# Four chained layers on one core: the product of step sizes and u moves from GpSimd to VectorE in the second state-space layer

## The chip, the cores and the metric

The kernel runs on one core of a Trainium2 chip. A core has five engines with a queue each: TensorE (PE in the profile; its weight loads are PEld), VectorE (DVE), ScalarE (ACT), GpSimd (POOL) and SyncE (SP), which here only issues transfers between the chip's memory (HBM) and the core's SBUF. Matrix products go to a second on-chip memory, PSUM, which TensorE writes and which VectorE and ScalarE read and write. Each engine works through its own instructions in order; between engines, semaphores hold an instruction back until what it reads is there and what it overwrites has been read.

The metric is the device time of one execution in microseconds (us). Lower is better.

## The reference

The input is eight images of 384 channels and 32 x 32 positions. Four layers follow one another: a state-space layer, a layer of deformable convolutions, a second state-space layer with layer norm and a small two-layer network behind it, and a layer of shifted Gaussian samples. The change is in the third of them, the second state-space layer. For each image its core is this recurrence over 1024 positions, with 768 inner channels d and 16 states n:

```python
dbc = xc @ x_proj_w.T
dt, Bm, Cm = jnp.split(dbc, [dt_rank, dt_rank + d_state], axis=-1)
dt = softplus(dt @ dt_proj_w.T + dt_proj_b)
A = -jnp.exp(A_log)
def step(h, inp):
    dt_t, B_t, C_t, u_t = inp
    dA = jnp.exp(dt_t[..., None] * A)
    h = dA * h + (dt_t * u_t)[..., None] * B_t[:, None, :]
    y = jnp.einsum('bdn,bn->bd', h, C_t)
    return (h, y)
```

The factor `dt_t * u_t`, called du below, is what the change is about: one elementwise product of the step sizes dt and the convolved input u.

## The kernel before

Everything is 32-bit floating point. `ssm_layer` runs both state-space layers. It splits each image into two halves of 512 positions, called steps: 16 steps in a layer, and the second step of an image carries the state of the first. The 768 inner channels are six tiles of 128. The work on one tile in one step is a block, and a block has eight units, 0 to 7. A unit holds 32 channels times 4 states on the 128 partitions and two further states in its 1024 columns. So a layer has 16 x 6 x 8 = 768 units, run strictly one after another.

One unit i does this:

- `inputs` (L539, GpSimd): db = du times B, 128 x 1024, three buffers. It is issued three units ahead, so it waits until the scan three units before it has released its buffer.
- `decays` (L531, ScalarE): da = exp(dt times A) into PSUM, two instructions of 512 columns, two buffers, issued two units ahead.
- `scan` (L551, VectorE): the recurrence over da and db. In units 0, 2 and 5 of a block its result goes to a tile hs in SBUF, otherwise it stays in PSUM in place of da.
- `with_c`: the product with C. Units 0, 2 and 5 do it on GpSimd (L562), the other five on VectorE (L564).
- `keep_last` (L557, ScalarE): in the first step of an image, the last state. In the second step, GpSimd adds the carried state to the first column (`carry` L514, `add_carry` L524).
- `read_out` (L574, TensorE): sums the states into y, one or two units later.

Around the units lies all other work of the layer, placed by hand. `plan` writes, for each step, four lists (act, dve, pool, pe) with one slot per unit, and fills them with the closing of the block before, the projections and the convolution of the next step, the output projection and the two-layer network of the step before, and the softplus of the block two ahead. In each unit the loop then issues, in this order: the slot's act list, the scan, VectorE's product with C, keep_last, the decays two units ahead, the dve list, the inputs three units ahead with their carry additions, GpSimd's product with C, the pool list, the pe list. On an engine, the order of issue is the order of execution. The transfers on SyncE's queue also run in order; their order is set when the kernel is built, from what they depend on.

The softplus of a tile is spread over one block: `dt_proj` (TensorE, slot 2), `soft_exp` (ScalarE, slot 3), `soft_rest` (VectorE L464, slot 4, writes the tile sp_e), `soft_ln` (ScalarE, slot 5), and in slot 6 `soft_sum` on GpSimd: two sums that finish dt (L472, L473), then the product with u, written over sp_e (L474). In slot 7 `spread` stores dt and du to HBM (L493, SyncE) and loads them back in the layout of the units (dtb and dub, four loads each, L498). The first reader of dub is the inputs of the next block's first unit, issued in slot 5 of the block between. The tiles dt, sp_e and sp_w have one buffer each.

The first state-space layer does not use `soft_sum`: there TensorE adds the three parts of the softplus in PSUM, ScalarE copies dt out, and VectorE multiplies the PSUM tile with u (`soft_du`, L488). The switch is `PE_SUM = (0,)`.

Other lines that the text speaks of: in the second state-space layer, `ln_scale` (L348, VectorE) scales the layer norm, `down_take` (L660, VectorE) adds the network's output to the residual x, `norm_stats` (L308, VectorE) takes statistics of a newly loaded x (L301), `fetch_in` (L280) loads the projection weights winr two units before their use. In the convolution layer, a set-up piece adds two one-column tiles on VectorE (L1107) while GpSimd subtracts weights (L1224, L1226).

Of the kernel before, what the change touches and what calls it, by code (L numbers as in the profile page):

```python
# [10 lines left out]
ALU = mybir.AluOpType  # L11
# [91 lines left out]
class Net:  # L103
# [112 lines left out]
    def ssm_layer(self, li, src, dst, shift=None):  # L216
        tc, nc, ins = self.tc, self.nc, self.ins
        mlp = li == 2
        gp_c = GP_C[li]
        pe_sum = li in PE_SUM  # L220
        sel = self.cols[:, Q_SEL : Q_SEL + IP]
        with ExitStack() as ctx:
# [210 lines left out]
            def load_bc(s, p):  # L433
                bc = s["bc"][p] = p2.tile([P, 2, 2, TS], F32, name="bc", tag="bc", bufs=3)
                for i in range(NI):
                    nc.sync.dma_start(
                        out=bc[i * IP : (i + 1) * IP].rearrange("p t q l -> p (t q) l"),
                        in_=s["bcd"][i, p].partition_broadcast(IP),
                    )
# [29 lines left out]
            def soft_sum(s, j):  # L469
                dt = s["dt", j]  # L470
                s["du", j] = du = s["e"]
                nc.gpsimd.tensor_tensor(dt, dt, s["e"], ALU.subtract)  # L472
                nc.gpsimd.tensor_tensor(dt, dt, s["w"], ALU.add)  # L473
                nc.gpsimd.tensor_tensor(du, dt, s["u"][:, j, :], ALU.mult)  # L474

# [215 lines left out]
            def plan(prev, s, nxt):  # L693
                act, dve, pool, pe = queues = [[[] for _ in range(T + NU)] for _ in range(4)]

                def put(q, t, fn, *args):
                    if not args or args[0]:
                        q[t].append((fn, *args))

                for j in range(ND):  # L700
                    t = NU * j
                    put(dve, t + 2, close, *((s, j - 1) if j else (prev, ND - 1)))
                    tz = TZ[j]
                    put(pe, tz - 2, fetch_in, s, ND + j)
                    put(pe, tz, z_proj, s, j)
                    put(act, TG[j], gate, s, j)

                    n, k = (s, j + 2) if j + 2 < ND else (nxt, j + 2 - ND)
                    put(pe, t + 2, dt_proj, n, k)
                    put(act, t + 3, soft_exp, n, k)  # L710
                    put(dve, t + 4, soft_rest, n, k)
                    put(act, t + 5, soft_ln, n, k)
                    if pe_sum:
                        put(pe, t + 6, soft_add, n, k)
                        put(act, t + 7, soft_take, n, k)
                        put(dve, t + 7, soft_du, n, k)
                    else:
                        put(pool, t + 6, soft_sum, n, k)
                    put(pool, t + 7, spread, n, k)
                for i, t in enumerate(TS2):  # L720
                    put(act, t, silu, nxt, 3 * i, 3 * i + 3)
# [3 lines left out]
                t = 0 if nxt else 14  # L725
# [67 lines left out]
            with tc.manual_schedule(engines=ENGINES):  # L793
                s = steps[0]
# [24 lines left out]
                states()  # L819
                for j in range(2):  # L820
                    for fn in (dt_proj, soft_exp, soft_rest, soft_ln) + (
                        (soft_add, soft_take, soft_du) if pe_sum else (soft_sum,)
                    ) + (spread,):
                        fn(s, j)
                    load_bc(s, j)
# [8 lines left out]
                for i, (s, j, m) in enumerate(units):  # L834
                    c, t = divmod(i, T)
                    if t == 0:
                        queues = plan(
                            steps[c - 1] if c else None, s, steps[c + 1] if c + 1 < len(steps) else None
                        )
                        for k, q in enumerate(over or ()):  # L840
                            for i0, items in enumerate(q):
                                queues[k][i0][:0] = items
                        act, dve, pool, pe = queues
                        over = [q[T:] for q in queues]
# [1313 lines left out]
```

## Time and profile before

| | us |
|---|---|
| median of 3 runs | 8728.45 (8723.46 to 8728.67) |
| the profiled execution | 8722.48 |
| its span, first to last instruction | 8720.7 |
| GpSimd's 96 products L474, each | 1.26 to 1.28 |

The second state-space layer begins at about 5300 us of the span and its last units end near 8460 us. In that stretch of 3160 us the engines were busy for 2573 us (TensorE), 2767 us (VectorE), 2260 us (ScalarE) and 2886 us (GpSimd).

How to read the lines further down: a group's line has the source line, the engine, the operation, output and inputs with their shape, the count, then the busy time and the mean nanoseconds of one, then the engine's idle time just before these instructions and what ended it. A line of the timeline has the start, the duration, the engine, the line and operation, output and inputs, and in brackets the idle time before it and what ended that. A line of the view by stretches has the stretch, its length, the busy time of TensorE, its weight loads, VectorE, ScalarE and GpSimd (with counts of instructions), the granted clock of TensorE, the busy share of the transfer engines and GB/s.

### The profile page before, as it was taken

What the parts mean: (1) busy time and instruction counts of PE and PEld (TensorE: products, weight loads), DVE (VectorE), ACT (ScalarE), POOL (GpSimd) and SP (SyncE); (2) the same over time, 40 slices, a digit from 0 to 9 for tenths busy, and PEclk for the clock granted to TensorE, in tenths of its full rate; (3) what the DMA queues carried; (4) which work ended last, traced back from release to release, by engine and by line L of the source; (5) the groups of instructions that cost most, each with busy time, mean ns of one, the idle gap of its engine ahead of it and who ended that gap; (6) DMA issues with size and microseconds to landing.
All of it is one profiled execution on the core that took longest, in us unless ns stands there. A gap on an engine that the chain in (4) does not pass through costs nothing. (4 is left out here: it accounts for less than half of the span.)

```text
span 8720.7 us, 91254 instructions
## 1 busy us (share of the span) xinstructions
PE 7387.2 (85%) x29688; PEld 3825.2 (44%) x29688; DVE 7519.7 (86%) x8480; ACT 5832.6 (67%) x9518; POOL 5569.8 (64%) x3383
## 2 busy tenths in 40 slices
PE   7888888888886899999999985788888888888878
PEld 2232233223222788888787871233333333333323
DVE  6999999999997788988988895888988989888884
ACT  6777777777774556666666665676767777776761
POOL 6999999999998000000000005998998989898984
PEclk8899899889987999999999997898998899999989
DMA  4555555555553754565456434565666666565657
GB/s 126 126 126 123 120 124 125 118 122 125 125 126 99 186 133 110 130 166 127 103 148 159 122 76 122 131 153 144 156 156 156 149 147 153 141 157 142 154 152 152
DMA packets 796928, 1179.29 MB, mean 135 GB/s; under 512 B 260402, under 2 KB 413010, under 8 KB 762648
## 3 DMA queue, kind: packets, MB, share of 16 engines
q1 hardware_dynamic: 739444, 1157.23, 54.0%
q10 hardware_dynamic: 55540, 10.05, 0.7%
q0 software_dynamic: 1456, 6.07, 0.2%
q8 instruction: 237, 3.88, 0.2%
q14 instruction: 251, 2.06, 0.1%
HBM read 984.15 MB, written 188.98 MB: 135 GB/s over the span
## 5 line engine op out<-in xcount | busy, mean ns | idle before, releaser
L539 POOL TENSOR_TENSOR db<-dub,bc 128x1024 f32<-128x1024 f32 x1536 | 3606.2, 2357 | 369.1 <-DVE hs L551 169.1
L531 ACT ACTIVATE da<-dtb,vec 128x512 f32<-128x512 f32 x3072 | 2122.2, 691 | 610.5 <-DVE hs L564 407.9
L551 DVE TENSOR_TENSOR_SCAN da<-da,db 128x1024 f32<-128x1024 f32 x960 | 2193.2, 2285 | 130.5 <-ACT da L531 86.1
L472 POOL TENSOR_TENSOR dt<-dt,sp_e 128x512 f32<-128x512 f32 x96 | 122.3, 1274 | 2468.0 <-DMA bc<-bcd 2463.7
L1803 PE MATMUL wacc<-fsm,fxk 128*128 128x195 f32 (+21 forms) x10624 | 1574.9, 306 | 98.6 <-DVE fsm L1766 69.4
L1803 PEld LDWEIGHTS wacc<-fsm,fxk 128*128 128x128 f32 x10624 | 1481.2, 195 | 232.8 <-DVE fsm L1766 140.5
L551 DVE TENSOR_TENSOR_SCAN hs<-da,db 128x1024 f32<-128x1024 f32 x576 | 1315.3, 2283 | 195.6 <-POOL db L524 84.0
L562 POOL TENSOR_TENSOR hs<-hs,bc 128x1024 f32<-128x1024 f32 x576 | 1357.0, 2356 | 34.1 <-ACT st L557 34.1
L564 DVE TENSOR_TENSOR hs<-da,bc 128x1024 f32<-128x1024 f32 x960 | 1175.6, 1225 | 122.4 <-PE y L574 72.9
L574 PE MATMUL y<-hs,cols 128*32 128x512 f32 x6144 | 968.6, 649 | 282.5 <-POOL hs L562 260.1
L1766 DVE TENSOR_TENSOR fsm<-fhy,fhx 128x585 f32<-128x585 f32 (+39 forms) x3136 | 1011.2, 389 | 85.8 <-PE wacc L1803 77.0
L1749 DVE TENSOR_TENSOR fxk<-fxt,fwk 128x1024 f32<-128x1024 f32 (+1 forms) x688 | 813.4, 1182 | 9.7 <-DMA fxt<-fxd 8.7
L1726 ACT ACTIVATE fhy<-fpyx,cell 128x416 f32<-128x416 f32 (+10 forms) x832 | 422.4, 580 | 315.2 <-DVE fsm L1766 315.2
L574 PEld LDWEIGHTS y<-hs,cols 128*32 128x32 f32 x6144 | 189.1, 113 | 1002.4 <-issue 507.7
L651 PE MATMUL ps_m<-hid,wm 128*128 128x512 f32 x1152 | 549.9, 632 | 61.9 <-ACT hid L646 27.8
L632 PE MATMUL ps_h<-t,wm 128*128 128x512 f32 x1152 | 533.4, 607 | 56.5 <-DVE sp_e L464 24.2
L1709 ACT ACTIVATE fhx<-fpyx,cell 128x352 f32<-128x352 f32 (+9 forms) x640 | 344.5, 610 | 294.6 <-DVE fsm L1766 264.1
L364 PE MATMUL ps_in<-xn,winr 128*128 128x512 f32 x576 | 326.4, 713 | 176.6 <-ACT xn L353 127.0
L651 PEld LDWEIGHTS ps_m<-hid,wm 128*128 128x128 f32 x1152 | 226.8, 203 | 395.1 <-issue 283.5
L632 PEld LDWEIGHTS ps_h<-t,wm 128*128 128x128 f32 x1152 | 217.0, 194 | 376.6 <-issue 275.6
L583 PE MATMUL ps_z<-xn,winr 128*128 128x512 f32 x576 | 301.5, 672 | 47.7 <-DVE sp_e L464 47.7
L606 PE MATMUL ps_o<-u,wm 128*128 128x512 f32 x576 | 279.9, 636 | 41.5 <-DMA wm<-in_wout 36.3
(239 smaller groups left out, 9885.4 us busy)
## 6 DMA issues: line engine op xcount, KB each, us to landing
dtb<-dtd SPq DMA_DIRECT2D x768, 256.0 KB
dub<-dtd SPq DMA_DIRECT2D x768, 256.0 KB
fpyx<-fposd SPq DMA_DIRECT2D x104, 1024.0 KB
fxt<-fxd SPq DMA_DIRECT2D x96, 1024.0 KB
wm<-in_w SPq DMA_DIRECT2D x96, 768.0 KB
bc<-bcd SPq DMA_DIRECT2D x256, 256.0 KB
x<-x SPq DMA_DIRECT2D x73, 768.0 KB
dtd<-dt SPq DMA_DIRECT2D x192, 256.0 KB
```

Of the source, the lines that this page charges most:

```text
L531: nc.scalar.activation(da[:, i, :], s["dtb", j][:, k, :], AF.Exp, scale=na[:, j, n + i : n + i + 1])
L539: nc.gpsimd.tensor_tensor(db, du, s["bc"][p][:, 0], ALU.mult)
L551: nc.vector.tensor_tensor_scan(h1, da1, db1, 0.0, ALU.mult, ALU.add)
L562: nc.gpsimd.tensor_tensor(s["hs", m], s["hs", m], c, ALU.mult)
L564: nc.vector.tensor_tensor(hs_tile(s, m), s["da", m], c, ALU.mult)
L574: nc.tensor.matmul(s["y"][k * IP : (k + 1) * IP, :], sel, s["hs", p * NSUB + k][:, i, :], start=mlp and p == 0 and i == 0, stop=p == NQP - ...
L632: nc.tensor.matmul(ps, s["w1", q][:, k, f * P : (f + 1) * P], s["t"][:, k, :], start=(k == 0), stop=(k == G - 1))
L651: nc.tensor.matmul(ps, s["w2", q][:, f, o * P : (o + 1) * P], s["hid", q][:, f, :], start=(f == 0), stop=(f == 3))
L1726: nc.scalar.activation(hy[:, at : at + (yb - ya) * W], s["pyx", j][:, 0, ya * W : yb * W], AF.Abs, bias=bias)
L1749: nc.vector.tensor_tensor(t[:, :n], x, wk[:, j : j + 1, :].to_broadcast([P, n, P]), ALU.mult)
L1766: nc.vector.tensor_tensor(self.sub(sm, at, [(r * w, n), (w, r), (1, w)]), self.sub(hy, hy_at[by] + xa, [(r * W, n), (W, r), (1, w)]), self ...
L1803: nc.tensor.matmul(a[:, ya - 4 * o : yb - 4 * o, xa:xb], k, self.sub(sm, sm_at[by], [(w, yb - ya), (1, w)]), start=o not in s["open"], sto ...
```

## The change

In the second state-space layer the third instruction of `soft_sum`, the product of dt and u, leaves GpSimd. A new function `soft_mul` issues it on VectorE with the same operands. In `plan` it goes into the dve list of slot 7, so it stands on VectorE after the scan and the product with C of the block's last unit and after nothing else of that slot. The two sums stay on GpSimd in slot 6. `spread` stays in slot 7 and now stores a du that VectorE wrote. Two more such products, before the first unit, move likewise: 96 in all.

```diff
                 nc.gpsimd.tensor_tensor(dt, dt, s["e"], ALU.subtract)
                 nc.gpsimd.tensor_tensor(dt, dt, s["w"], ALU.add)
-                nc.gpsimd.tensor_tensor(du, dt, s["u"][:, j, :], ALU.mult)
+
+            def soft_mul(s, j):
+                du = s["du", j]
+                nc.vector.tensor_tensor(du, s["dt", j], s["u"][:, j, :], ALU.mult)
...
                         put(pool, t + 6, soft_sum, n, k)
+                        put(dve, t + 7, soft_mul, n, k)
                     put(pool, t + 7, spread, n, k)
...
-                        (soft_add, soft_take, soft_du) if pe_sum else (soft_sum,)
+                        (soft_add, soft_take, soft_du) if pe_sum else (soft_sum, soft_mul)
```

## The prediction

> **What bounds the kernel now.** I read the engines' shares and the slices of the page first, then stretches of the second state-space layer, its groups of instructions, and the timeline of VectorE and GpSimd around one softplus.
>
> ```profile
> PE 7387.2 (85%) x29688; PEld 3825.2 (44%) x29688; DVE 7519.7 (86%) x8480; ACT 5832.6 (67%) x9518; POOL 5569.8 (64%) x3383
> ...
> DVE  6999999999997788988988895888988989888884
> ...
> POOL 6999999999998000000000005998998989898984
> ```
>
> GpSimd works only in the two state-space layers, and there as hard as VectorE. Two stretches of the second one, in the view by stretches:
>
> ```profile
> 6400.00:6600.00 200.00, 174.78 (x514) 63.86 (x513) 181.88 (x130) 145.80 (x241) 187.27 (x114) 0.91 0.60 147
> 6600.00:6800.00 200.00, 163.51 (x487) 62.88 (x486) 171.99 (x133) 143.30 (x243) 175.68 (x110) 0.90 0.62 151
> ```
>
> VectorE is the third busy column (86 to 91%), GpSimd the fifth (88 to 94%), TensorE the first (82 to 87%). No engine is full: they hand work to each other in a ring and each waits a little. Groups of 5400 to 8200 us:
>
> ```profile
> L539 POOL TENSOR_TENSOR db<-dub,bc 128x1024 f32<-128x1024 f32 x681 | 1599.0, 2356 | 173.4 <-DVE hs L551 113.4 <-DVE da L551 31.6 <-DMA dub<-dtd 27.6
> ...
> L472 POOL TENSOR_TENSOR dt<-dt,sp_e 128x512 f32<-128x512 f32 x85 | 108.3, 1274 | 0.0
> L473 POOL TENSOR_TENSOR dt<-dt,sp_w 128x512 f32<-128x512 f32 x85 | 107.8, 1269 | 6.7
> L474 POOL TENSOR_TENSOR sp_e<-dt,u 128x512 f32<-128x512 f32 x85 | 107.7, 1267 | 6.7
> ```
>
> GpSimd's own waits end mostly on VectorE's scan L551: it has caught up and waits for a free db buffer. So GpSimd sets the pace less than VectorE does. The place itself, GpSimd then VectorE, in the fourth image:
>
> ```profile
> 6627.57 2.35 POOL L539 TENSOR_TENSOR db<-dub,bc 128x1024 f32<-128x1024 f32 x1 [3.14 <-DVE hs L551]
> 6629.88 2.38 POOL L562 TENSOR_TENSOR hs<-hs,bc 128x1024 f32<-128x1024 f32 x1
> 6632.20 2.37 POOL L539 TENSOR_TENSOR db<-dub,bc 128x1024 f32<-128x1024 f32 x1
> 6634.52 1.27 POOL L472 TENSOR_TENSOR dt<-dt,sp_e 128x512 f32<-128x512 f32 x1
> 6635.87 1.26 POOL L473 TENSOR_TENSOR dt<-dt,sp_w 128x512 f32<-128x512 f32 x1
> 6637.22 1.26 POOL L474 TENSOR_TENSOR sp_e<-dt,u 128x512 f32<-128x512 f32 x1
> ```
> ```profile
> 6627.41 2.27 DVE L551 TENSOR_TENSOR_SCAN da<-da,db 128x1024 f32<-128x1024 f32 x1
> 6629.71 1.23 DVE L564 TENSOR_TENSOR hs<-da,bc 128x1024 f32<-128x1024 f32 x1
> 6630.86 2.29 DVE L551 TENSOR_TENSOR_SCAN da<-da,db 128x1024 f32<-128x1024 f32 x1
> 6633.25 1.23 DVE L564 TENSOR_TENSOR hs<-da,bc 128x1024 f32<-128x1024 f32 x1
> 6634.39 2.28 DVE L551 TENSOR_TENSOR_SCAN hs<-da,db 128x1024 f32<-128x1024 f32 x1
> 6639.06 2.30 DVE L551 TENSOR_TENSOR_SCAN da<-da,db 128x1024 f32<-128x1024 f32 x1 [2.39 <-ACT da L531]
> ```
>
> The sixth unit's scan ends at 6627.5 and releases GpSimd, which needs 9.6 us to the end of its second sum (L473, 6637.1). VectorE needs 7.0 us to the end of the eighth unit's product (L564, 6634.5), after which the change puts the multiply. Both paths start from the same scan, so this gap of 2.7 us does not close when VectorE is late.
>
> **The change part by part.** *Removed:* 96 GpSimd multiplies of 1.267 us, 122 us of its time. It is worth something only where VectorE waits for GpSimd; from 5200 us on, scans of hs waited 34.0 us for the carry additions (L524) and 27.7 us for db (L539), so at most 62 us. It also lets GpSimd catch up in two blocks of an image where it still ran 0.8 to 0.9 us late.
>
> *Added wait:* in 94 blocks VectorE's queue stands at the multiply until L473 is done. Behind it stand the next scans (so the decays of ScalarE that need their PSUM buffer, the db products that need their SBUF buffer, TensorE's read-out), and at two places of an image the layer norm's scaling (L348) or a residual addition (L660). I read the gap g, from the end of that last L564 to the end of L473, off the timeline in the twelve blocks of the fourth image (the two late ones set to 2.65).
>
> *Added instruction:* a multiply of 128x512 from two SBUF tiles. No VectorE row of this layer reads two SBUF tiles; those with two inputs have one in PSUM. The lower bound is such a row, L594 at 0.69 us. The upper bound is that it first waits out the GpSimd product that starts with it. GpSimd's next product (L539) needs nothing from L473: where GpSimd's instruction is independent of the one before it, it starts 0.04 us before that one's end, while VectorE starts 0.03 us after a GpSimd end that it waited for. So GpSimd is first by 0.07 us, and the multiply would end at 2.35 - 0.04 + 0.69 = 3.0 us after L473. The nearest row to this is elsewhere in the trace, the only adds of VectorE from two SBUF tiles beside a busy GpSimd (L1107, one element per partition):
>
> ```profile
> 2823.36 8.97 POOL L1226 TENSOR_TENSOR firw<-firw 128x1078 f32<-128x1078 f32 x4
> 2832.29 2.29 POOL L1232 DMA_DIRECT2D fwd<-firw  x3
> ...
> 2827.27 5.09 DVE L1107 TENSOR_TENSOR fobk<-fobk,fob 128x1 f32<-128x1 f32 x1 [12.80 <-DMA fobk<-in_c_cols]
> ```
>
> One element took 5.09 us and ended when GpSimd's row of subtractions did, at 2832.3. Its twin at 2809.53 took 0.52 and ended with a GpSimd instruction too. So I take the upper end, 3.0 us; GpSimd pauses after that one product, since the next db needs the buffer of the scan behind the multiply.
>
> The Trainium skill, "SBUF — State Buffer", section "Who interferes with whom", says that a VectorE instruction with two SBUF inputs and a GpSimd one that reads SBUF exclude each other, and that the later one waits for the whole instruction of the earlier. The 5.09 us spanned three subtractions, which is longer than that rule gives. By the rule the hold ends with the one product; by the row it may also take in the carry addition that follows at once in every second step (0.08 + 0.19 us, 47 blocks, 13 us in all). The rule speaks against the change, and either way the sum moves by less than its uncertainty.
>
> *What is absorbed.* A delay of VectorE is hidden where its next wait ends on something that was not itself waiting for the delayed scans. Per block: gap, cost (gap + 3.0), hidden, left, in us:
>
> 1: 2.65, 5.65, 1.4 (a wait for db), 4.3
> 2: 2.65, 5.65, 1.7 (GELU and its tables on ScalarE, 1.2, then some of a read-out, since L348 and with it TensorE come later), 4.0
> 3: 1.37, 4.4, 2.0 (SiLU and tables), 2.4
> 4: 2.67, 5.7, 2.8 (SiLU; then ScalarE itself waits for the late scan before GELU), 2.9
> 5: 0.03, 3.0, 2.7 (hidden layer on TensorE), 0.3
> 6: 2.07, 5.1, 0.7 (L660 waits for TensorE). The 1.8 and 6.1 us after it hide nothing: x's second load stands on SP's queue ahead of dtb and dub and waits for the statistics L308, which move too. Left 4.4
> 7: 1.64, 4.6, 3.1, 1.5
> 8: 3.25, 6.25, 2.8 (GELU, read-out), 3.4
> 9: 1.95, 4.95, 1.7 (SiLU), 3.3
> 10: 3.26, 6.3, 2.3, 4.0
> 11: 1.73, 4.7, 3.9, 0.8
> 12: 1.48, 4.5, 0.9 (L660), 3.6
>
> The costs sum to 61, the hidden to 26, and 35 us an image are left. Over 94 blocks, 94 / 12 x 35 = 273, taken as +270 us.
>
> *The moved transfers.* The store of du and, behind it, eight loads (dtb, dub) wait for the multiply: du is ready 3.0 instead of 1.35 us after L473, and SP's queue stands 1.65 us longer. Their first reader is six units (some 24 us) later, so nothing, except in block 6, where the x load in the same queue is later still. In each image a few winr loads stand on the other side of these stores; they are issued two units (some 8 us) ahead. If that cover went, TensorE would wait as it does now for winr, 11.8 us in two waits.
>
> The profiled execution took 8722.48 us (span 8720.7), 6 us under the median of the runs. 8722.5 + 270 + 6 = 8998 us.
>
> **The rivals.** *No hold* (chance 0.18): VectorE reads both tiles beside GpSimd and the multiply costs 0.69 + 0.03. For: 0.07 us is a narrow race. Against: L1107. Costs 33.4 us an image; the same waits hide 23, since smaller delays fit into them; left 10.3, so 94 / 12 x 10.3 = 80 us: 8808.
>
> *Nothing hidden* (0.10): ScalarE and TensorE follow VectorE through the ring and the waits come back after it. For: GpSimd and ScalarE wait for L551 and L564 at most places. Against: GELU, SiLU and their tables run before the scan that they are said to wait for. 94 / 12 x 61 = 478 us: 9206.
>
> *GpSimd's relief decides* (0.04, faster): if L473 ended before the eighth unit's L564, there would be no wait, and VectorE's 62 us of waits for GpSimd would go: 8667. The relief of 1.27 us would have to exceed the gap; it does in one block of twelve, and it comes after L473, not before.
>
> *All fits into idle time* (0.02): VectorE idles 3 us a block now, against a cost of 5.
>
> **How the numbers follow.** My forecast has 0.66. Faster by over 0.2% (17 us, about what a measurement of this kernel can tell from no change) has 0.04, within it 0.02, slower 0.94. The range runs from just under the no-hold case, 8790, to 9150, most of the way to nothing hidden; the forecast's own is 8900 to 9100.
>
> **What would show it.** VectorE's new line: 96 instructions of about 3 us for the forecast, 0.69 for no hold, with waits for L473 before them that sum to about 94 x 2.1 = 195 us. GpSimd's time falls by 122 us and it waits after the first db behind L473. Layer 2 grows by some 35 us an image, block 6 by 4 us. I am wrong if the new line's mean is under 1 us, or if ScalarE's and TensorE's idle time grows by as much as VectorE's delay.

## The result and the profile after

The changed kernel takes 8977.61 us in the median (8973.81 to 8978.81, 4 runs), against 8727.11 us before in the same measurement (8723.46 to 8728.67, 4 runs): a ratio of 1.0287, 95% interval 1.0269 to 1.0305. It is 250 us slower; 270 were forecast. The profiled execution has a span of 8975.6 us.

The first line of the page, the engines' busy time, and two stretches, one of 200 us as shown of before and the whole second state-space layer (columns: stretch, length, busy time of TensorE, its weight loads, VectorE, ScalarE and GpSimd with counts, granted clock, transfer share, GB/s):

```profile
PE 7412.8 (83%) x29688; PEld 3829.9 (43%) x29688; DVE 7770.4 (87%) x8576; ACT 5844.8 (65%) x9518; POOL 5470.3 (61%) x3287
```
```profile
6400.00:6600.00 200.00, 152.97 (x448) 58.49 (x447) 175.32 (x131) 130.12 (x207) 163.87 (x121) 0.89 0.57 141
...
5300.00:8710.00 3410.00, 2594.91 (x7590) 954.12 (x7589) 3012.23 (x2110) 2273.15 (x3767) 2779.43 (x1675) 0.88 0.56 136
```

VectorE has 251 us more busy time than before in all. GpSimd has 100 us less and falls from nine tenths of the layer to 82%. From its first scan to its last product with C the layer takes 3397.1 us in place of 3145.5, 252 more; outside it the two profiles differ by 3 us. An image, from its first scan to the next image's first, takes 428.3 us in place of 396.0 (mean of the second to the seventh).

The new line, by its instructions:

```profile
L477 DVE TENSOR_TENSOR sp_e<-dt,u x96: 692/2820/2845, 5309.3 to 8666.0; 128x512 f32<-128x512 f32 x96
its engine sat idle before it (us, times) until:
  POOL dt L473: 225.9, 89
```

Shortest, median and longest are 0.69, 2.82 and 2.85 us (only the two ahead of the first unit take 0.69; no GpSimd instruction runs beside them), and VectorE stood idle 226 us before these 96 instructions until GpSimd's second sum was done. Neither number existed before. The place in the fourth image, VectorE and then GpSimd:

```profile
6749.35 1.22 DVE L567 TENSOR_TENSOR hs<-da,bc 128x1024 f32<-128x1024 f32 x1
6753.29 2.83 DVE L477 TENSOR_TENSOR sp_e<-dt,u 128x512 f32<-128x512 f32 x1 [2.72 <-POOL dt L473]
6756.04 2.28 DVE L554 TENSOR_TENSOR_SCAN hs<-da,db 128x1024 f32<-128x1024 f32 x1
```
```profile
6750.64 1.28 POOL L472 TENSOR_TENSOR dt<-dt,sp_e 128x512 f32<-128x512 f32 x1
6751.99 1.26 POOL L473 TENSOR_TENSOR dt<-dt,sp_w 128x512 f32<-128x512 f32 x1
6753.21 2.36 POOL L542 TENSOR_TENSOR db<-dub,bc 128x1024 f32<-128x1024 f32 x1
6758.40 2.34 POOL L542 TENSOR_TENSOR db<-dub,bc 128x1024 f32<-128x1024 f32 x1 [2.82 <-DVE hs L554]
```

Read them together. L473 ends at 6753.25. GpSimd's next db product began 0.04 us earlier, the multiply begins 0.03 us after. The db product ends at 6755.57, the multiply 0.55 us later, at 6756.12. Then the scan runs, and only its end at 6758.32 lets GpSimd go on: it waits 2.82 us, where it ran on before.

The groups of 5400 to 8400 us that answer to those shown before:

```profile
L542 POOL TENSOR_TENSOR db<-dub,bc 128x1024 f32<-128x1024 f32 x673 | 1582.2, 2355 | 501.2 <-DVE hs L554 394.2 <-DVE da L554 55.9 <-DMA dub<-dtd 30.2
L554 DVE TENSOR_TENSOR_SCAN da<-da,db 128x1024 f32<-128x1024 f32 x421 | 960.8, 2282 | 23.0 <-ACT da L534 23.0
...
L477 DVE TENSOR_TENSOR sp_e<-dt,u 128x512 f32<-128x512 f32 x84 | 237.1, 2823 | 193.0 <-POOL dt L473 192.5
```

GpSimd's waits for VectorE have more than tripled (113 to 394 us for the scans of hs). VectorE's waits for ScalarE before its scans of da have shrunk. The line of before, in the window of 5400 to 8200 us:

```profile
L551 DVE TENSOR_TENSOR_SCAN da<-da,db 128x1024 f32<-128x1024 f32 x425 | 972.0, 2287 | 104.7 <-ACT da L531 80.1 <-POOL sp_e L474 13.6 <-ACT st L557 5.2
```

So 80 us became 23, and the scans of hs, which waited 42 us for the decays, no longer wait for them. (The 13.6 us are waits for the decays too: each of these scans starts 0.09 us after a decay's end.) This is idle time that hid a part of the delay.

### The profile page after: what moved, and what is told of

The parts are those of the page before. It is cut to its first block, busy times and chain, and to the rows that moved or that the text cites. A ratio compares the mean times of both kernels' runs of the same rounds, so it can differ in the third digit from the quotient of the medians.

```text
span 8975.6 us, 91226 instructions
## 1 busy us (share of the span) xinstructions
PE 7412.8 (83%) x29688; PEld 3829.9 (43%) x29688; DVE 7770.4 (87%) x8576; ACT 5844.8 (65%) x9518; POOL 5470.3 (61%) x3287
## 5 line engine op out<-in xcount | busy, mean ns | idle before, releaser
L477 DVE TENSOR_TENSOR sp_e<-dt,u 128x512 f32<-128x512 f32 x96 | 266.7, 2778 | 226.5 <-POOL dt L473 225.9
L609 PE MATMUL ps_o<-u,wm 128*128 128x512 f32 x576 | 306.0, 682 | 123.2 <-DVE u L597 81.8
```

## The experiments

Every run was compared with the kernel before on its own chip (8722 to 8726 us). A diff is against the changed kernel where the text does not say otherwise. The first four take the change apart.

**The product left out.**

```diff
             def soft_mul(s, j):
-                du = s["du", j]
-                nc.vector.tensor_tensor(du, s["dt", j], s["u"][:, j, :], ALU.mult)
+                pass
```

> The product of dt and u is left out on both engines: the tile that should hold du keeps the softplus part e, so the output is not the reference's. It shows what GpSimd's relief of 1.27 us a block is worth by itself. My theory: little, since GpSimd mostly waits for VectorE's scans; 0 to 62 us faster than the kernel before (VectorE's waits for GpSimd were 62 us), I expect about 20 faster, 8707. A rival by which GpSimd's time sets the pace expects up to 94 x 1.27 = 119 us faster, 8608.

Measured: 8735.24 us against 8722.72, ratio 1.0015 (1.0005 to 1.0025): 12.5 us slower with less work. This missed. The wait that grew is TensorE's for projection weights; first this run, then the kernel before:

```profile
PE ps_in L364 <- DMA winr<-in_win: 95.9, 18, 11.1
```
```profile
PE ps_in L364 <- DMA winr<-in_win: 11.8, 2, 6.6
```

Without a product on GpSimd or VectorE the stores of dt and du depend on other instructions, and the build puts the winr loads at other places of SyncE's queue. A later run keeps them in place.

**Only the wait.** One column, and the next unit's decays (PSUM) in place of u.

```diff
-            def soft_mul(s, j):
+            def soft_mul(s, j, now=None):
                 du = s["du", j]
-                nc.vector.tensor_tensor(du, s["dt", j], s["u"][:, j, :], ALU.mult)
+                other = now["da", 0][:, 0, :] if now else s["u"][:, j, :]
+                nc.vector.tensor_tensor(du[:, 0:1], s["dt", j][:, 0:1], other[:, 0:1], ALU.mult)
...
-                        put(dve, t + 7, soft_mul, n, k)
+                        put(dve, t + 7, soft_mul, n, k, s if j + 1 < ND else nxt)
```

> VectorE's multiply is cut to one column, and its second operand is a tile in PSUM (the decays of the next unit, needed there at once anyway) in place of u; du is wrong but for nothing in the timing. What is left is the wait for GpSimd's second sum L473. Theory (wait, hold by the GpSimd product that starts with it, own work): the new line takes about 0.1 to 0.15 us, the waits for L473 stay at about 2.1 us a block, and the kernel is about 45 us slower than before, 8772. Rival, the wait alone makes the loss: about as slow as the changed kernel, 8950 or more.

Measured: 8767.99 us, 45 us slower, ratio 1.0050 (1.0033 to 1.0067). The line's group has the same wait as the changed kernel, and takes 0.16 us:

```profile
L478 DVE TENSOR_TENSOR sp_e<-dt,da 128x1 f32<-128x1 f32 x94 | 14.6, 156 | 226.2 <-POOL dt L473 226.2
```

So 226 us of new waiting, with the moved transfers, cost only 45 us of the kernel's time. That the wait alone makes the loss falls.

**The whole multiply with one operand in PSUM.**

```diff
-                nc.vector.tensor_tensor(du, s["dt", j], s["u"][:, j, :], ALU.mult)
+                other = now["da", 0][:, 0, :] if now else s["u"][:, j, :]
+                nc.vector.tensor_tensor(du, s["dt", j], other, ALU.mult)
```

> The full multiply, 128x512, but its second operand is a PSUM tile (the next unit's decays) in place of u, so du is wrong. VectorE reads one SBUF tile only. Theory: no hold by GpSimd, the new line takes 0.69 us in place of 2.82, and the kernel is about 80 us slower than before, 8808. Rival, that the multiply's place and wait make the loss whatever it reads: 8978 as the changed kernel.

Measured: 8807.78 us, 85 us slower, ratio 1.0099 (1.0082 to 1.0116).

```profile
L478 DVE TENSOR_TENSOR sp_e<-dt,da 128x512 f32<-128x512 f32 x94 | 64.7, 688 | 223.9 <-POOL dt L473 223.7
```

The same place, wait, shape and output as in the changed kernel, but 0.69 us in place of 2.82, and 165 us less loss (85 in place of 250): what the second operand's memory decides. All of SyncE's transfers stand in the same order as in the changed kernel, here, in the run before and in the next two, so that order is not what differs.

**One column of two SBUF tiles.**

```diff
-                nc.vector.tensor_tensor(du, s["dt", j], s["u"][:, j, :], ALU.mult)
+                nc.vector.tensor_tensor(du[:, 0:1], s["dt", j][:, 0:1], s["u"][:, j, 0:1], ALU.mult)
```

> The multiply with both operands in SBUF as in the changed kernel, but one column instead of 512 (the rest of du is left wrong). Theory, a hold until the GpSimd product that is under way ends: the new line still takes about 2.3 us, and the kernel is about 225 us slower than before, 8952. Rival, the two engines share the reading and the multiply is slowed in proportion to its size: 0.1 to 0.2 us, and about 45 us slower, 8772.

Measured: 8919.25 us, 197 us slower, ratio 1.0224 (1.0206 to 1.0241).

```profile
L477 DVE TENSOR_TENSOR sp_e<-dt,u x96: 160/2287/2312, 5304.1 to 8617.0; 128x1 f32<-128x1 f32 x96
```

One element per partition takes 2.29 us beside GpSimd; with a PSUM operand it took 0.16. The time does not go with the size: it is a hold, not a sharing. The loss is 28 us under the theory's 225 and far from the rival's 45.

**GpSimd lets VectorE go first.** This and the kernels with a later multiply compute all of du.

```diff
                 nc.vector.tensor_tensor(du, s["dt", j], s["u"][:, j, :], ALU.mult)
+                turn = p1.tile([P, 1], F32, name="turn")
+                nc.gpsimd.tensor_tensor(turn, du[:, 0:1], du[:, 0:1], ALU.add)
```

> The changed kernel, and GpSimd gets a one-column addition that reads the finished du, between its second sum and its next db product; the output stays the reference's. GpSimd thus cannot start the db product before the multiply is done. Theory, the multiply loses a race of 0.07 us and is then held for a whole GpSimd product: the new line falls to about 0.6 to 0.7 us, GpSimd pays about 0.9 us a block for it, and the kernel comes near the version with a PSUM operand (8808): 8815. Rival, the hold comes from somewhere else than that GpSimd product: the line stays at 2.8 us and the time at 8978 or above.

Measured: 8797.71 us, 74 us slower, ratio 1.0083 (1.0066 to 1.0100). The multiply, and GpSimd's queue at one place:

```profile
L477 DVE TENSOR_TENSOR sp_e<-dt,u x96: 691/692/694, 5310.1 to 8487.8; 128x512 f32<-128x512 f32 x96
```
```profile
6640.37 1.27 POOL L473 TENSOR_TENSOR dt<-dt,sp_w 128x512 f32<-128x512 f32 x1
6642.45 0.19 POOL L479 TENSOR_TENSOR turn<-sp_e 128x1 f32<-128x1 f32 x1 [0.81 <-DVE sp_e L477]
6642.59 2.37 POOL L544 TENSOR_TENSOR db<-dub,bc 128x1024 f32<-128x1024 f32 x1
```

GpSimd now stands 0.81 us and does one more small instruction in every block, and the kernel is 180 us faster than the changed one. The hold is that of the one db product which wins the start by 0.07 us.

**Two slots later.**

```diff
-                        put(dve, t + 7, soft_mul, n, k)
-                    put(pool, t + 7, spread, n, k)
+                        put(dve, t + 9, soft_mul, n, k)
+                    put(pool, t + (7 if pe_sum else 9), spread, n, k)
```

> The changed kernel with the multiply, and the stores and loads behind it, two slots later: after the second scan of the next block. By then the second sum L473 is long done, so the wait for it goes; GpSimd is busy with a db or an hs product at an arbitrary point, so a hold of some half of 2.35 us on average stays, with a spread of the line's duration from 0.7 to 3 us. Theory, costs of about 1.2 + 0.6 us a block of which two thirds are hidden: about 55 us slower than before, 8780. Rival, the loss is VectorE's added work and hold alone, and the wait was hidden anyway: about 8930.

Measured: 8790.20 us, 67 us slower, ratio 1.0073 (1.0056 to 1.0089).

```profile
L477 DVE TENSOR_TENSOR sp_e<-dt,u x96: 680/1844/2852, 5310.5 to 8488.9; 128x512 f32<-128x512 f32 x96
```

The wait is gone, the hold is now the rest of whatever product GpSimd has under way, and it never exceeds one, though GpSimd's products follow each other without a gap. One place, where a db product of GpSimd ends at 6639.66:

```profile
6638.20 2.00 DVE L477 TENSOR_TENSOR sp_e<-dt,u 128x512 f32<-128x512 f32 x1
```
```profile
6639.60 2.79 POOL L565 TENSOR_TENSOR hs<-hs,bc 128x1024 f32<-128x1024 f32 x1
```

The hs product had begun 0.06 us before that end, yet the multiply finished first, and the hs product took 2.79 us in place of 2.36. The same shows in 54 blocks, where the next db or hs product took 2.78 to 2.86 us. A new cost comes in: over the run GpSimd waited 183 us for dub (63 before), as du is stored later.

**SyncE's transfers in the order of the program text**, in the kernel before and in the changed one:

```diff
-            with tc.manual_schedule(engines=ENGINES):
+            with tc.manual_schedule(engines=ENGINES | {mybir.EngineType.SP} if mlp else ENGINES):
```

> The kernel before, with SyncE's transfers in the second state-space layer issued in the order of the program text instead of an order set from their dependences. It is the partner of the next run. What it does by itself no theory here says; between 8680 and 8830, I expect 8740.

> The changed kernel with SyncE's transfers in the order of the program text. Against the run before it, the change acts with no transfer changing place. Theory, the loss is wait, hold and work on VectorE, and the moved winr loads add little (TensorE waited 38 us for winr after the change, 12 us before): 215 to 250 us slower than its partner. Rival, the moved loads make a large part of the loss: less than 190 us slower than its partner.

Measured: 9000.02 and 9194.26 us, 277 and 471 us over the kernel before; the change costs 194 us between them. Both expectations missed their ranges, and the pair decides little: in this order TensorE's matmuls wait 253 and 213 us for winr (12 in the kernel before), so a part of VectorE's delay probably falls into a new stall. It shows only that the order of that queue can cost more than the change.

**GpSimd's product cut to one column**, in the kernel before, with every transfer in place:

```diff
-                nc.gpsimd.tensor_tensor(du, dt, s["u"][:, j, :], ALU.mult)
+                nc.gpsimd.tensor_tensor(du[:, 0:1], dt[:, 0:1], s["u"][:, j, 0:1], ALU.mult)
```

> The kernel before, with GpSimd's product cut to one column (the rest of du is left wrong): 0.19 in place of 1.27 us, 94 x 1.08 = 101 us less of GpSimd's time, every instruction and every transfer at its old place. The version without any product also moved winr loads on SyncE's queue, and TensorE waited 90 us for them in place of 12. Theory, GpSimd's relief is worth something small that those loads hid: 5 to 60 us faster than before, I expect 25 faster, 8700. Rival, the relief is worth nothing at all: 8720 to 8730. Second rival, GpSimd sets the pace: 8640 or less.

Measured: 8714.18 us against 8722.29, ratio 0.9989 (0.9980 to 0.9998). So 101 us less of GpSimd's time are worth 8 us, at the low end of what was expected; by the interval, 2 to 17 us. From 5200 us on, the scans of hs wait 43.0 us for GpSimd in place of 61.7, but 54.7 us in place of 42.1 for the decays: most of what GpSimd no longer holds up then waits for ScalarE. TensorE's wait for winr is 2.8 us here, 11.8 in the kernel before. The run without any product differs by 0.19 us more relief a block and by the order of the transfers, and is 21 us slower.

**One slot later.**

```diff
-                        put(dve, t + 7, soft_mul, n, k)
-                    put(pool, t + 7, spread, n, k)
+                        put(dve, t + 8, soft_mul, n, k)
+                    put(pool, t + (7 if pe_sum else 8), spread, n, k)
```

> The changed kernel with the multiply, and the stores and loads behind it, one slot later, after the first scan of the next block. That scan, 2.28 us, now runs in the gap before L473; the multiply then finds the db product under way that began with the end of L473. Theory, the multiply ends at the same time as in the changed kernel, 2.9 us after L473, but VectorE has lost 2.3 us less in each block: near the version without a hold, 80 us slower than before, 8803; the line takes between 0.7 and 2.8 us. Rival, a later du delays dub and GpSimd waits for it: 8850 or more.

Measured: 8746.38 us, 24 us slower, ratio 1.0027 (1.0016 to 1.0039); the rival of a late dub (8850 or more) falls, and the theory's 8803 was 57 us too high. The mechanism was as described: in the fourth image the multiply ended 2.85 to 2.92 us after L473 in all twelve blocks, as in the changed kernel. But a scan of 2.28 us is done in that time. The stores stand later as well, and TensorE's waits for winr before ps_in, 43.5 us in the changed kernel, are gone (one of 17.8 us stands elsewhere); how much of the gain is theirs was not separated.

**One slot later, and GpSimd lets VectorE go first.**

```diff
+                    if mlp and m == 0 and i and i + 2 < len(units):
+                        inputs(*units[i + 2])
+                        add_carry(*units[i + 2])
-                    if i + 3 < len(units):
+                    if i + 3 < len(units) and not (mlp and m == NU - 1):
                         inputs(*units[i + 3])
```

beside the later slot and the one-column addition `turn` of the runs above. The db product that GpSimd issued at the eighth unit's place, behind the sums, is issued one unit later, behind `turn`.

> The multiply one slot later, after the next block's first scan, and GpSimd's third db product of that block issued behind it, after a one-column addition that reads du. So VectorE neither waits for L473 for long nor is held; the output stays the reference's. Theory, VectorE pays 0.7 us a block (1.7 us in two blocks of an image), most of it hidden, GpSimd's relief is worth some 8 us: 0 to 40 us slower than the kernel before, I expect 8735. Rival, GpSimd pays for standing still and the ring slows: 8770 or more. It beats both kernels only if all of VectorE's new work is hidden.

Measured: 8717.19 us against 8726.10, ratio 0.9988 (0.9979 to 0.9997): 9 us faster than the kernel before, outside the range expected, and 262 us faster than the changed one. The multiply's group:

```profile
L477 DVE TENSOR_TENSOR sp_e<-dt,u 128x512 f32<-128x512 f32 x96 | 64.8, 675 | 35.8 <-POOL dt L473 35.8
```

It beats both kernels, though by no more than the relief alone is worth (8 us). That fits the expectation's reading, that all of VectorE's new work is hidden; but some transfers stand in another order than in the kernel before, and none of TensorE's waits for winr is left (11.8 us before), so what the 9 us consist of is not shown.

**The changed kernel again**, on the last run's chip:

> The changed kernel once more, on the chip of the last run, so that the hold can be read against its neighbours: 8970 to 8982, 2.87% over the kernel before.

Measured: 8979.62 us against 8726.10, ratio 1.0286 (1.0271 to 1.0302), 253.5 us slower.

## Why the prediction was right

The change's 250 us (253.5 in the second measurement), by what each run adds to the one before it. The transfers stand in the first row as in the kernel before, in the other three as in the changed one:

| step | run | over the kernel before, us | added, us |
|---|---|---|---|
| relief of GpSimd | product cut to a column | -8 | -8 |
| wait for L473, and moved transfers | one column, PSUM | 45 | 53 |
| own work, 0.69 us | whole, PSUM | 85 | 40 |
| hold by a GpSimd product | changed kernel | 250 | 165 |

**The place and the gap.** VectorE waits for L473 after the eighth unit's product, and the gap does not close although VectorE is late: in the fourth image the twelve gaps after are 2.68, 2.65, 1.35, 2.68, 0.05, 2.08, 1.64, 3.25, 1.95, 3.25, 1.73 and 1.46 us, each within 0.03 of the table's. The waits sum to 226 us, not 195: the first image and the last step, which the table did not hold, have longer ones (together 21 us), and the two multiplies ahead of the first unit wait 5 us.

**The hold.** The upper end was right: the multiply ends 2.85 us after L473 where 3.0 was worked out. The 0.15 us is that it has only 0.55 left to do once it is let in, not 0.69. The prediction let the hold end with that one product because GpSimd then pauses; the multiply two slots later shows that no pause is needed. The run with the one-column addition shows the race that the prediction named: when GpSimd cannot start first, the line takes 0.692 us in all 96 cases. The trace agrees here with what the Trainium skill, "SBUF — State Buffer", "Who interferes with whom", says on a VectorE instruction with two SBUF inputs: it waits for one whole GpSimd instruction, 2.29 us for a single element. The longer wait of L1107, which the prediction weighed against that rule, was no guide to the length: no multiply here took over 2.85 us. But it is no accident either: in all 14 traces of this case that addition is held, for 3.67 to 5.48 us, until 0.02 us after the last of GpSimd's row of subtractions, over one or two whole ones besides the one under way. There one instruction was not the limit, and the measurement stands against the rule as stated.

**The no-hold rival** was priced at 80 us; the two kernels that are that case, with a PSUM operand and with GpSimd yielding, take 85 and 74 us.

**What was hidden.** Forecast 35 us left an image, measured 33.4 in the fourth. By block, forecast and measured growth in us (from one block's last L564 to the next's): 4.3 and 4.1; 4.0 and 2.2; 2.4 and 3.7; 2.9 and 2.4; 0.3 and 0.0; 4.4 and 5.3; 1.5 and 1.0; 3.4 and 3.1; 3.3 and 3.0; 4.0 and 4.0; 0.8 and 1.4; 3.6 and 3.3. The sum is nearer than its parts. That it came so near is partly luck: single blocks are off by up to 1.8 us either way. In block 6 nothing was hidden, as said: the load of x is issued at 6834.57, ahead of dub at 6837.00, and a wait of 7.1 us for the read-out stands where 6.1 stood. The forecast's excess of 20 us is spread: the first seven images grew by 33.0 us in the mean in place of 35, and the last, where ten blocks have a multiply, by 21 in place of 29.

**Where a step failed.** The winr loads that come to stand on the other side of the stores of dt and du were costed at nothing, since they are issued two units ahead. That was wrong in kind, though small here. In block 3 of every image from the second on, TensorE waits 3.1 to 5.3 us for winr after the change and not before; over the run its matmuls of ps_in wait 43.5 us against 11.8. Block 3 of these images grew by 3.4 us in the mean where 2.4 was forecast, and by 1.3 in the first image, where that wait was there before too. So the wait is probably what the forecast missed there, some 1 us an image; no run isolates it. The 21 us between the two runs without a full product are a measure of what such a move can cost, not of what it cost here.

**GpSimd's time.** It fell by 100, not 122 us. Most of the difference is that the carry addition behind the db product is itself held by the multiply in the second step of an image: 47 additions take 0.52 us, and the 384 have a mean of 234 ns, where it was 193 before.

**Readings that were loose.** VectorE's idle time in the fourth image is 3.8 us a block, not 3. GpSimd does not work in the two state-space layers alone: it has the subtractions of L1107's place and 102 us in the last layer. And the last sign of being wrong says little: with unchanged work, TensorE's and ScalarE's idle time had to grow by about as much as the layer did (228 and 237 us by the stretches shown). VectorE's delay, its waits of 226 us and 267 us of multiplies, is twice that; half of it was hidden.

The Trainium skill, "GPSIMD Engine Reference", "Engine selection", sends an elementwise product to VectorE, as GpSimd is about twice as slow. The instruction alone agrees (0.69 against 1.27 us), the kernel does not: at this place the faster engine takes 2.8 us.

## What to carry to other kernels

Before a product moves from GpSimd to VectorE, look where its operands lie and what GpSimd starts at the same moment: with both operands in SBUF it was held here until GpSimd's current product ended (and L1107 until a whole row of subtractions had), and the hold shows as busy time, not as a wait. Then look for the place where VectorE has other work to do in that time: one scan later, with GpSimd made to start second, turned a loss of 250 us into a gain of 9. And do not take relief of an engine as worth its own time: here 101 us of it were worth 8.

## What the runs showed of the hardware

A single-element VectorE instruction took 2.29 us beside GpSimd and 0.16 us with one operand in PSUM. For the multiply the hold ended with the GpSimd product under way: at an arbitrary point of GpSimd's unbroken queue (two slots later) it took at most 2.85 us, so the waiting VectorE went in ahead of GpSimd's next product. The hold works in both directions: the carry addition that came 0.08 us after the db product took 0.52 in place of 0.19 us while the multiply ran, and a db or hs product that began just before the multiply was let in took 2.78 to 2.86 us in place of 2.36. Why the one-element addition L1107 is not let in between two subtractions, in any of the 14 traces, stays open; it was not tried.
